# State-space block on one Trainium2 core: weighted sums in one phase a unit later, full-height small matmuls, and normalisation on ScalarE

## The chip, the cores and the metric

The kernel runs on one core of a Trainium2 chip. The core has five engines with a queue of instructions each, which it executes in order: TensorE (PE in the profile; PEld is its loading of stationary operands), VectorE (DVE), ScalarE (ACT), GpSimd (POOL) and SyncE (SP), which here issues the DMA transfers. Engines wait for each other by semaphores. SBUF is the working memory of 128 partitions; PSUM, in banks of 512 fp32 numbers per partition, takes the results of TensorE. The metric is the device time of one execution in microseconds.

## The reference

The input `x` is 4 x 4096 x 512 in fp32. A Mamba block with a residual is followed by a spectral layer with a residual:

```python
x = x + mamba(layernorm(x))        # D_INNER 1024, 16 states, conv of 4 taps, DT_RANK 32
x = x + ffn(layernorm(x))          # ifft(fft(x) @ w), real part, plus bias

# mamba, per time step:
u, z = split(x @ W_in.T);  u = silu(conv4(u) + conv_b)
dt_r, B, C = split(u @ W_x.T)      # 32, 16, 16
dt = softplus(dt_r @ W_dt.T + b_dt)
h  = exp(dt * A) * h + (dt * u) * B      # one state of 16 numbers for each of 1024 channels
y  = sum over the states of h * C
out = ((y + u * D) * silu(z)) @ W_out.T
```

The part that matters here is `h` (a recurrence along time for each channel and state) and `y`, the sum of `h` over the 16 states, weighted by `C`.

## The kernel before, in words

The 4 x 4096 rows are cut into 32 chunks of T = 512 time steps. In a chunk the 1024 channels are 8 blocks `d` of 128 partitions, and the 16 states are 4 groups `q` of four. One **unit** is one (chunk, d, q): there are 32 x 8 x 4 = 1,024 of them, and the main loop goes through them in order.

Four steps make a unit:

- `scans` (L451 on): POOL forms `bh` = du * B for 128 channels x 512 steps x 4 states (L455). For each of the four states ACT computes the decay `a` = exp(dt * A) into one of two PSUM tiles (L97, by way of L459), and DVE scans along time (L461). POOL then keeps the last column as `carry` (L464). Three `bh` buffers rotate (BH = 3).
- `contract` (L467 on), one unit behind the scans: the 512 steps are taken in four blocks `tt` of 128 steps. TensorE transposes four slices of 32 steps x 4 states into one of two PSUM tiles `tr` (L479); ACT copies them to SBUF as `hT` (L481); four matmuls with the mask of `C`, 32 columns wide each, sum over the states into `yT` (L483). These four stand at different columns of the array (`tile_position`). An fp32 matmul of this kind shows as two instructions in the trace, a transpose as one. A `yT` accumulates over the four `q` of a `d`; there is one PSUM buffer for it. The state tile `bh` comes free after its last transpose.
- `gate` (L499 on), after the fourth `q` of a block: ACT copies `yT` to `ys` (L505), TensorE transposes it back (L510), DVE adds `u * D` (L512), which releases the `ur` tile, and POOL multiplies by the gate `zr` (L519) that SP has loaded (L503).
- `prep` (L419 on), issued six units ahead: SP loads `ur` (L422); TensorE computes dt's input `v` from a full matmul (L426) and a correction with 32 rows (L427); ACT and POOL make softplus and `du` of it (L429 to L447).

`make_C` (L412 on) forms the masks of `C` for the next chunk with a 32-row matmul (L414) and a product on DVE (L416). `normalize` (L214 on) computes mean and variance on DVE, the inverse root on ACT and small DVE operations (L228 to L230), and applies them on POOL (L232). It serves the 128 input tiles (four at a time, in `load_norm`) and the 128 tiles of the second layernorm (one at a time, in `out_norm`).

All other work is "background": the input projection of the next chunk (`project`, matmuls at L332, weights by SP), output projection and spectral layer of the chunk before (L539, L573). In each unit `run_step` goes through four ticks. In each tick it takes one step of `contract` and one of `scans`, then steps of pending gates, then as much background work as two budgets allow (L686 to L722). A scheduler at build time then fixes the order on each engine from the dependencies and its own estimates; `add_manual_dep` adds an order between two instructions without a semaphore.

The loop calls the units like this:

```python
for i in range(NCH):
    for d in range(ND):
        for q in range(NQ):
            ...
            run_step((i, d, q), prev, share)
            prev = (i, d, q)
run_step(None, prev, (0.0, 0.0))
```

Of the kernel before, what the change touches and what calls it, by code (L numbers as in the profile page):

```python
# [8 lines left out]
F32 = mybir.dt.float32  # L9
F32R = mybir.dt.float32r  # L10
AF = mybir.ActivationFunctionType
ALU = mybir.AluOpType
# [4 lines left out]
P = 128  # L17
T = 512
M = 512
KM = M // P  # L20
DI = 1024
ND = DI // P
NS = 16
NQ = 4
# [7 lines left out]
XL = 2  # L32
AB = 2
PH = 2
HT = 4
BH = 3
CB = 4
TMP = 4
# [27 lines left out]
def tile_mamba_block(  # L66
# [108 lines left out]
    wx = cst.tile([P, ND, P], F32, name="wx")  # L175
    rc = cst.tile([P, 3], F32, name="rc")
    wv = cst.tile([P, DI], F32R, name="wv")
    wl = cst.tile([96, DI], F32R, name="wl")
    selt = wl[64:96, 0 : NQ * P].rearrange("s (q p) -> s q p", p=P)
    bias_bc = cst.tile([P, M], F32, name="bias_bc")  # L180
    dmask = cst.tile([P, 32], F32, name="dmask")
    carry = cst.tile([P, ND, NS], F32, name="carry")
# [11 lines left out]
    def consts2():  # L194
        nc.sync.dma_start(A, a_log)
        lut(A, A, AF.Exp)
        nc.vector.tensor_scalar(A, A, -1.0, None, ALU.mult)
        nc.sync.dma_start(dsk, d_skip)
        nc.sync.dma_start(dmask, diag)
        nc.sync.dma_start(bias_bc, bias.to_broadcast([P, M]))  # L200
        wvr = p_bh.tile([P, 2, DI], F32, name="wvr", tag="bh")
        nc.gpsimd.memset(wvr[:, 0, :], 0.0)
        nc.sync.dma_start(wvr[0:32, 0, :], w_dt_t)
        nc.sync.dma_start(wvr[32:64, 0, :], w_dt_t)
        nc.sync.dma_start(wvr[112:113, 0, :], b_dt)
        nc.sync.dma_start(wvr[113:114, 0, :], b_dt)
        nc.sync.dma_start(wvr[64:96, 1, 0 : NQ * P], sel.rearrange("s q p -> s (q p)"))
        nc.vector.tensor_copy(wl[64:96, 0 : NQ * P], wvr[64:96, 1, 0 : NQ * P])
        wvh = p_bh.tile([P, 2, DI], F32R, name="wvh", tag="bh")
        nc.scalar.activation(wvh[:, 0, :], wvr[:, 0, :], AF.Copy)  # L210
        nc.vector.scalar_tensor_tensor(wv, wvh[:, 0, :].bitcast(F32), rc[:, 2:3], wvr[:, 0, :], ALU.mult, ALU.add)
        nc.vector.tensor_tensor(wl[0:32, :], wvr[0:32, 0, :], wvh[0:32, 0, :].bitcast(F32), ALU.subtract)

    def normalize(srcs, dsts):  # L214
        n = len(srcs)
        st = p_sm.tile([P, n, 6], F32, name="st", tag=f"st{n}", bufs=SMB)
        mv = p_sm.tile([P, n, 2], F32, name="mv", tag=f"mv{n}", bufs=SMB)
        for k, src in enumerate(srcs):
            nc.vector.bn_stats(st[:, k, :], src)
            nc.vector.bn_aggr(mv[:, k, :], st[:, k, :])  # L220
        ve = p_sm.tile([P, n], F32, name="ve", tag=f"ve{n}", bufs=SMB)
        nc.vector.tensor_scalar(ve, mv[:, :, 1], EPS, None, ALU.add)
        rs = p_sm.tile([P, n], F32, name="rs", tag=f"rs{n}", bufs=SMB)
        lut(rs, ve, AF.Ln)
        lut(rs, rs, AF.Exp, scale=-0.5)
        for k in range(n):
            v, r = ve[:, k : k + 1], rs[:, k : k + 1]
            nc.vector.tensor_scalar(v, v, r, r, ALU.mult, ALU.mult)  # L228
            nc.vector.tensor_scalar(v, v, -0.5, 1.5, ALU.mult, ALU.add)
            nc.vector.tensor_scalar(r, r, v, None, ALU.mult)  # L230
        for k, (src, dst) in enumerate(zip(srcs, dsts)):
            nc.gpsimd.tensor_scalar(dst, src, mv[:, k, 0:1], rs[:, k : k + 1], ALU.subtract, ALU.mult)  # L232

    S = {i: {} for i in range(-1, NCH + 1)}

# [175 lines left out]

    def make_C(i, q):  # L412
        pc = ps_ph.tile([P, T // 32, 32], F32, name="pc", tag="ph")
        nc.tensor.matmul(pc, selt[:, q, :], S[i]["stk"][64:96, :], start=True, stop=True)  # L414
        cm = p_C.tile([P, T // 32, 32], F32, name="cm")
        nc.vector.tensor_tensor(cm, pc, dmask.unsqueeze(1).to_broadcast([P, T // 32, 32]), ALU.mult)  # L416
        S[i]["C", q] = cm

    def prep(i, d):  # L419
        st = S[i]  # L420
        u = p_ur.tile([P, T], F32, name="ur")
        nc.sync.dma_start(u, st["us"][d])  # L422
        st["u", d] = u
        v = ps_ph.tile([P, T], F32, name="v", tag="ph")
        ds = slice(d * P, (d + 1) * P)
        nc.tensor.matmul(v, wv[:, ds], st["stk"], start=True, stop=False)  # L426
        nc.tensor.matmul(v, wl[0:32, ds], st["stk"][0:32, :], start=False, stop=True)  # L427
        e = p_tmp.tile([P, T], F32, name="e", tag="tmp")
        nc.scalar.activation(e, v, AF.Abs)  # L429
        r = p_tmp.tile([P, T], F32, name="r", tag="tmp")  # L430
        nc.scalar.activation(r, v, AF.Relu)  # L431
        lut(e, e, AF.Exp, scale=-1.0)
        yield
        w = p_tmp.tile([P, T], F32, name="w1", tag="tmp")
        nc.gpsimd.tensor_scalar(w, e, 1.0, -1.0, ALU.add, ALU.add)  # L435
        l = p_tmp.tile([P, T], F32, name="l", tag="tmp")
        lut(l, e, AF.Ln, bias=1.0)
        yield
        nc.gpsimd.tensor_tensor(e, e, w, ALU.subtract)  # L439
        yield  # L440
        nc.gpsimd.tensor_tensor(l, l, e, ALU.add)
        yield
        dt = p_dt.tile([P, T], F32, name="dt")
        nc.gpsimd.tensor_tensor(dt, r, l, ALU.add)
        yield
        du = p_dt.tile([P, T], F32, name="du")
        nc.gpsimd.tensor_tensor(du, dt, u, ALU.mult)  # L447
        st["dt", d] = dt
        st["du", d] = du
# [14 lines left out]
            nc.gpsimd.tensor_copy(carry[:, d, 4 * q : 4 * q + 4], bh[:, T - 1, :])  # L464
        st["h", d, q] = bh

    def contract(i, d, q):  # L467
        st = S[i]
        bh = st.pop(("h", d, q))
        if q == 0:  # L470
            st["y", d] = ps_y.tile([P, T // P, P], F32, name="yT")
            st["first"] = {}
        yT = st["y", d]
        cm = st["C", q]
        for tt in range(T // P):
            tr = ps_tr.tile([P, 4, P], F32, name="tr")
            for j in range(4):
                t0 = (tt * 4 + j) * 32
                nc.tensor.transpose(tr[:, j, :], bh[:, t0 : t0 + 32, :].rearrange("p t s -> p (t s)"), ident)  # L479
            hT = p_hT.tile([P, 4, P], F32, name="hT")  # L480
            nc.scalar.activation(hT, tr, AF.Copy)  # L481
            for j in range(4):
                ins = nc.tensor.matmul(  # L483
                    yT[32 * j : 32 * j + 32, tt, :],
                    cm[:, tt * 4 + j, :],
                    hT[:, j, :],
                    start=(q == 0 and tt == 0),
                    stop=(q == NQ - 1),
                    skip_group_check=True,
                    tile_position=(0, 32 * j),  # L490
                )
                if q == 0:
                    if tt == 0:
                        st["first"][j] = ins.ins
                    else:
                        tc.add_manual_dep(ins.ins, st["first"][j].name, NOSYNC, reason="bank start first")
            yield

    def gate(i, d):  # L499
        st = S[i]  # L500
# [184 lines left out]

    def run_step(cur, prev, share):  # L686
        gens = []
        if prev is not None:
            gens.append(contract(*prev))
        if cur is not None:  # L690
            gens.append(scans(*cur))
        if SC1:
            gens.reverse()
        if prev is not None and prev[1] == ND - 1 and prev[0] + 1 < NCH:
            make_C(prev[0] + 1, prev[2])
        for _ in range(4):
            tick[0] += 1
            if PSTEP and tick[0] % PSTEP == 0:
                for g in list(soon):
                    if next(g, "end") == "end":  # L700
                        soon.remove(g)
            for what in SLOT:
                if what == "m":
                    for g in gens:
                        next(g, None)
                elif what == "g":
                    for g in list(late):
                        if next(g, "end") == "end":
                            late.remove(g)
                elif what == "a":  # L710
                    bga.advance(share[0] / 4)
                else:
                    bgb.advance(share[1] / 4)
        for g in gens:
            next(g, None)
        if cur is not None and cur[1] == ND - 1 and cur[0] + 1 < NCH:
            load_B(cur[0] + 1, cur[2])
        if prev is not None and prev[2] == NQ - 1:
            i, d = prev[0], prev[1]
            bgb.until(lambda: ("z", d) in S[i])  # L720
            bga.until(lambda: len(yz_free) >= 2)
            late.append(gate(i, d))  # L722
# [5 lines left out]
# [3 lines that stand above are left out]
# [13 lines left out]
                run_step((i, d, q), prev, share)  # L744
                prev = (i, d, q)
    run_step(None, prev, (0.0, 0.0))
    for g in late:
        run(g)
    for g in (bgb, bga):
# [66 lines left out]
```

## Time and profile before

| | us |
|---|---|
| median of 3 runs | 8955.14 (8951.78 to 8959.92) |
| the profiled execution, its own time | 8950.2 |
| its span, first to last instruction | 8948.4 |
| busy: PE / POOL / DVE / ACT | 7853.7 / 6985.1 / 6652.0 / 6460.5 |
| mean granted TensorE clock | 0.938 |
| DMA, mean over the span | 152 GB/s |

A row of the groups names the line, the engine, the operation, the tiles written and read, the shape and the number of instructions; then their busy time together and the mean duration of one in ns; then the idle time of the engine just before them, with what ended it. A row of the waits gives who waited for whom, the total, how often and the longest. A row of the timeline gives start and length of a stretch of equal instructions. Matmuls overlap each other in these rows, so costs are read from one start to the next rather than from the lengths.

### The profile page before, as it was taken

Reading aid. Unit: us, or ns where it says so; the run is one execution under the profiler, and the core shown is the slowest. Engines: PE = TensorE matmul, PEld = TensorE weight load, DVE = VectorE, ACT = ScalarE, POOL = GpSimd, SP = SyncE. Lnnn points to the kernel's source line nnn. Section 1 sums busy time; section 2 is a strip of 40 time slices with the busy share of each in tenths; the row PEclk is TensorE's granted clock in tenths of the full one; section 3 lists DMA queues with packets and bytes.
Section 4 is the critical chain, followed back from the end, with each engine's and each line's share of the span. In section 5 each row is a group of like instructions: output and inputs, shape, how many; then the busy total and the mean of one; then the engine's idle time right before and its main releaser. Section 6 shows DMA issues by size and latency. Waiting matters only on the chain. (4 is left out here: it accounts for less than half of the span.)

```text
span 8948.4 us, 163408 instructions
## 1 busy us (share of the span) xinstructions
PE 7853.7 (88%) x62400; PEld 4812.5 (54%) x62400; DVE 6652.0 (74%) x7776; ACT 6460.5 (72%) x11199; POOL 6985.1 (78%) x4484
## 2 busy tenths in 40 slices
PE   7998888888888888898888898888988888888888
PEld 4555555555555555555555555555555555555554
DVE  5677777777777777777777777777777777777776
ACT  5777777777777777777677776777767777777775
POOL 5777778777778787887777887788778788778786
PEclk9999999999999999999999999999999999999999
DMA  7544444444444444444444444444444344444444
GB/s 236 161 161 155 154 139 144 150 156 154 143 145 154 151 160 144 144 147 159 155 150 142 143 152 154 158 143 149 148 151 161 132 151 147 162 155 152 142 148 145
DMA packets 615138, 1363.45 MB, mean 152 GB/s; under 512 B 126066, under 2 KB 138482, under 8 KB 597972
## 3 DMA queue, kind: packets, MB, share of 16 engines
q1 hardware_dynamic: 614356, 1353.00, 46.0%
q8 instruction: 494, 8.09, 0.4%
q14 instruction: 288, 2.36, 0.1%
HBM read 1171.38 MB, written 181.40 MB: 151 GB/s over the span
## 5 line engine op out<-in xcount | busy, mean ns | idle before, releaser
L461 DVE TENSOR_TENSOR_SCAN bh<-a,carry,bh 128x512 f32<-128x512 f32 x3584 | 4397.1, 1270 | 918.2 <-POOL bh L455 556.0
L455 POOL TENSOR_TENSOR bh<-du,bq 128x2048 f32<-128x2048 f32 x1024 | 3970.1, 3879 | 710.3 <-PE tr L479 675.8
L97 ACT ACTIVATE a<-dt,A 128x512 f32<-128x512 f32 x4096 | 2822.9, 694 | 1056.2 <-DVE bh L461 1038.0
L481 ACT ACTIVATE hT<-tr 128x512 f32<-128x512 f32 x4096 | 2388.0, 594 | 862.7 <-PE tr L479 847.4
L479 PE MATMUL tr<-ident,bh 128*128 128x128 f32 x16384 | 2813.4, 299 | 220.9 <-ACT hT L481 110.5
L479 PEld LDWEIGHTS tr<-ident,bh 128*128 128x128 f32 x16384 | 1844.7, 148 | 1067.5 <-issue 906.9
L483 PE MATMUL yT<-hT,cm 128*32 128x128 f32 x32768 | 1804.4, 295 | 565.3 <-ACT hT L481 507.7
L483 PEld LDWEIGHTS yT<-hT,cm 128*32 128x32 f32 x32768 | 662.1, 110 | 1732.1 <-ACT hT L481 948.5
L332 PE MATMUL pp<-xh,w 128*128 128x512 f32 x4096 | 1467.7, 421 | 17.1 <-ACT r L431 6.6
L539 PE MATMUL po<-wo,yz 128*128 128x512 f32 x2048 | 957.3, 597 | 22.0 <-DVE xr L576 9.1
L332 PEld LDWEIGHTS pp<-xh,w 128*128 128x128 f32 x4096 | 812.2, 199 | 220.0 <-issue 14.0
L332 PE MATMUL pp<-xl,w 128*128 128x512 f32 x2048 | 836.6, 409 | 7.2 <-DVE xl L296 7.1
L461 DVE TENSOR_TENSOR_SCAN bh<-a,bh 128x512 f32<-128x512 f32 x512 | 594.9, 1209 | 167.0 <-POOL bh L455 91.3
L464 POOL COPY carry<-bh 128x4 f32<-128x4 f32 x896 | 182.0, 203 | 532.0 <-DVE bh L461 506.5
L435 POOL TENSOR_SCALAR w<-e 128x512 f32<-128x512 f32 x256 | 495.1, 1934 | 116.1 <-ACT e L97 116.0
L343 DVE SCALAR_TENSOR_TENSOR u<-pp,cw,u 128x509 f32<-128x509 f32 (+2 forms) x768 | 565.7, 737 | 11.6
L519 POOL TENSOR_TENSOR yz<-g,zr 128x256 f32<-128x256 f32 x512 | 368.8, 741 | 250.8 <-DVE g L512 193.1
L539 PEld LDWEIGHTS po<-wo,yz 128*128 128x128 f32 x2048 | 359.2, 191 | 332.2 <-issue 291.9
L332 PEld LDWEIGHTS pp<-xl,w 128*128 128x128 f32 x2048 | 408.1, 199 | 91.7 <-DVE xl L296 11.1
L573 PE MATMUL pf<-g,x1t 128*128 128x512 f32 x1024 | 370.9, 443 | 85.6 <-DMA g<-g_split 51.9
L512 DVE SCALAR_TENSOR_TENSOR g<-ur,dsk,yt 128x512 f32<-128x512 f32 x256 | 188.2, 735 | 249.9 <-ACT hT L481 106.6
L439 POOL TENSOR_TENSOR e<-e,w 128x512 f32<-128x512 f32 x256 | 330.1, 1289 | 40.3 <-ACT l L97 38.5
(86 smaller groups left out, 6814.3 us busy)
## 6 DMA issues: line engine op xcount, KB each, us to landing
wo<-w_out_t SPq DMA_DIRECT2D x516, 512.0 KB, 4.9
g<-g_split SPq DMA_DIRECT2D x512, 512.0 KB, 4.0
w<-w_split SPq DMA_DIRECT2D x496, 512.0 KB, 3.4
bq<-bsc SPq DMA_DIRECT2D x128, 1024.0 KB, 4.9
xr<-x SPq DMA_DIRECT2D x256, 256.0 KB, 3.2
usc<-u SPq DMA_DIRECT2D x256, 256.0 KB, 2.9
ur<-usc SPq DMA_DIRECT2D x256, 256.0 KB, 2.7
zsc<-u SPq DMA_DIRECT2D x256, 256.0 KB, 2.5
```

The costliest lines, as they stand in the source:

```text
L97: ins = nc.scalar.activation(out_, in_, func, **kw)
L332: nc.tensor.matmul(ps, w[:, wsel, k, :], xt[:, k, :], start=(n == 0), stop=(n == 3 * KM - 1))
L343: nc.vector.scalar_tensor_tensor(u[:, j:], ps[:, : T - j], cw[:, d, 3 - j : 4 - j], u[:, j:], ALU.mult, ALU.add)
L435: nc.gpsimd.tensor_scalar(w, e, 1.0, -1.0, ALU.add, ALU.add)
L455: nc.gpsimd.tensor_tensor(bh, st["du", d].unsqueeze(2).to_broadcast([P, T, 4]), st["B", q], ALU.mult)
L461: nc.vector.tensor_tensor_scan(bh[:, :, j], a, bh[:, :, j], init, ALU.mult, ALU.add)
L479: nc.tensor.transpose(tr[:, j, :], bh[:, t0 : t0 + 32, :].rearrange("p t s -> p (t s)"), ident)
L481: nc.scalar.activation(hT, tr, AF.Copy)
L483: ins = nc.tensor.matmul(yT[32 * j : 32 * j + 32, tt, :], cm[:, tt * 4 + j, :], hT[:, j, :], start=(q == 0 and tt == 0), stop=(q == NQ - 1 ...
L519: nc.gpsimd.tensor_tensor(yz, g[:, hs], zr[:, hs], ALU.mult)
L539: nc.tensor.matmul(po, yz_of(i, d, tt), wo[:, d % 2, :], start=(d == d0), stop=(d == d1 - 1))
L573: nc.tensor.matmul(pf, a[:, k, :], g[:, b, :], start=(k == 0 and m == 0), stop=(k == KM - 1 and m == 2))
```

## The change

Three things change. (1) `contract` is split. It still transposes and copies a unit's four blocks, but keeps the four `hT` tiles in `held`; a new function `weigh` does the sixteen weighted sums of the unit before, all in a row, after the first block's transposes. Manual dependencies place them after that block and ahead of the second block's transposes. `hT` has five buffers in place of four. `gate` and `make_C` follow the unit that was weighed, so they move a unit later, and one more step stands at the end. (2) The constants `selt` and `wl` are filled with zeros to 128 rows, and the matmuls at L414 and L427 take all 128 rows of `stk`. (3) `normalize` applies mean and inverse root with an Identity activation on ACT, scale `r` and bias `-m * r`; the bias is one more small DVE operation for each tile.

```diff
-HT = 4
+HT = 5
@@
-    wl = cst.tile([96, DI], F32R, name="wl")
-    selt = wl[64:96, 0 : NQ * P].rearrange("s (q p) -> s q p", p=P)
+    wl = cst.tile([P, DI], F32R, name="wl")
+    selt = cst.tile([P, NQ, P], F32R, name="selt")
@@ consts2
+        nc.gpsimd.memset(wvr[:, 1, 0 : NQ * P], 0.0)
         nc.sync.dma_start(wvr[64:96, 1, 0 : NQ * P], sel.rearrange("s q p -> s (q p)"))
-        nc.vector.tensor_copy(wl[64:96, 0 : NQ * P], wvr[64:96, 1, 0 : NQ * P])
+        nc.vector.tensor_copy(selt.rearrange("s q p -> s (q p)"), wvr[:, 1, 0 : NQ * P])
...
-        nc.vector.tensor_tensor(wl[0:32, :], wvr[0:32, 0, :], wvh[0:32, 0, :].bitcast(F32), ALU.subtract)
+        nc.gpsimd.memset(wvr[:, 1, :], 0.0)
+        nc.vector.tensor_tensor(wvr[0:32, 1, :], wvr[0:32, 0, :], wvh[0:32, 0, :].bitcast(F32), ALU.subtract)
+        nc.vector.tensor_copy(wl, wvr[:, 1, :])
@@ normalize
-            nc.gpsimd.tensor_scalar(dst, src, mv[:, k, 0:1], rs[:, k : k + 1], ALU.subtract, ALU.mult)
+            m, r = mv[:, k, 0:1], rs[:, k : k + 1]
+            nc.vector.tensor_scalar(m, m, r, -1.0, ALU.mult, ALU.mult)
+            nc.scalar.activation(dst, src, AF.Identity, scale=r, bias=m)
@@ make_C, prep
-        nc.tensor.matmul(pc, selt[:, q, :], S[i]["stk"][64:96, :], start=True, stop=True)
+        nc.tensor.matmul(pc, selt[:, q, :], S[i]["stk"], start=True, stop=True)
...
-        nc.tensor.matmul(v, wl[0:32, ds], st["stk"][0:32, :], start=False, stop=True)
+        nc.tensor.matmul(v, wl[:, ds], st["stk"], start=False, stop=True)
@@ contract
+    held = []
+
+    def weigh(after):
+        i, d, q, blocks = held.pop()
+        st = S[i]
+        if q == 0:
+            st["y", d] = ps_y.tile([P, T // P, P], F32, name="yT")
+        yT = st["y", d]
+        cm = st["C", q]
+        prev = after
+        for tt, hT in enumerate(blocks):
+            for j in range(4):
+                ins = nc.tensor.matmul(
+                    yT[32 * j : 32 * j + 32, tt, :],
...
+                ).ins
+                if prev is not None:
+                    tc.add_manual_dep(ins, prev.name, NOSYNC, reason="one phase")
+                prev = ins
+        return prev, (i, d, q)
+
+    def contract(i, d, q, done):
+        st = S[i]
+        bh = st.pop(("h", d, q))
+        blocks = []
+        after = None
+        for tt in range(T // P):
+            tr = ps_tr.tile([P, 4, P], F32, name="tr")
+            for j in range(4):
+                t0 = (tt * 4 + j) * 32
+                ins = nc.tensor.transpose(tr[:, j, :], bh[:, t0 : t0 + 32, :].rearrange("p t s -> p (t s)"), ident).ins
+                if after is not None:
+                    tc.add_manual_dep(ins, after.name, NOSYNC, reason="one phase")
+                    after = None
+            hT = p_hT.tile([P, 4, P], F32, name="hT")
+            nc.scalar.activation(hT, tr, AF.Copy)
+            blocks.append(hT)
+            if tt == 0 and held:
+                after, unit = weigh(ins)
+                done.append(unit)
             yield
+        held.append((i, d, q, blocks))
@@ run_step
-        if prev is not None and prev[1] == ND - 1 and prev[0] + 1 < NCH:
-            make_C(prev[0] + 1, prev[2])
+        if prev is None and held:
+            done.append(weigh(None)[1])
...
-        if prev is not None and prev[2] == NQ - 1:
-            i, d = prev[0], prev[1]
+        for i, d, q in done:
+            if d == ND - 1 and i + 1 < NCH:
+                make_C(i + 1, q)
+            if q < NQ - 1:
+                continue
             bgb.until(lambda: ("z", d) in S[i])
             bga.until(lambda: len(yz_free) >= 2)
             late.append(gate(i, d))
@@
     run_step(None, prev, (0.0, 0.0))
+    run_step(None, None, (0.0, 0.0))
```

More of the change, by code (lines that the diff above doesn't have):

```diff
@@ L465, in scans @@
         st["h", d, q] = bh
-    def contract(i, d, q):
+    held = []
+    def weigh(after):
+        i, d, q, blocks = held.pop()
         st = S[i]
-        bh = st.pop(("h", d, q))
         if q == 0:
             st["y", d] = ps_y.tile([P, T // P, P], F32, name="yT")
-            st["first"] = {}
         yT = st["y", d]
         cm = st["C", q]
[L475 to L481, printed above, removed]
+        prev = after
+        for tt, hT in enumerate(blocks):
             for j in range(4):
@@ L490, in contract @@
                     tile_position=(0, 32 * j),
[L491 to L496, printed above, removed]
+                ).ins
[22 more added lines that the diff above has]
+                done.append(unit)
             yield
+        held.append((i, d, q, blocks))
     def gate(i, d):
@@ L687, in run_step @@
         gens = []
+        done = []
         if prev is not None:
-            gens.append(contract(*prev))
+            gens.append(contract(*prev, done))
         if cur is not None:
```

## The prediction

> **What bounds the kernel now.** I read the page's busy shares first, then the waits of TensorE, then the timeline of TensorE in steady state, then the groups of the lines that the diff touches.
>
> ```profile
> PE 7853.7 (88%) x62400; PEld 4812.5 (54%) x62400; DVE 6652.0 (74%) x7776; ACT 6460.5 (72%) x11199; POOL 6985.1 (78%) x4484
> ```
>
> No engine is full, but TensorE is nearest to it: 7854 of 8948 us, alike in all slices. There are 1,024 units (32 chunks x 8 channel blocks x 4 state groups), so a unit takes 8948.4 / 1024 = 8.74 us, and of that TensorE is busy 7.67, POOL 6.82, DVE 6.50 and ACT 6.31.
>
> What TensorE waits for, longest first (total us, times, longest):
>
> ```profile
> PE yT L483 <- ACT hT L481: 507.7, 452, 5.6
> PE tr L479 <- ACT hT L481: 110.5, 85, 5.6
> PE tr L479 <- DVE bh L461: 106.7, 88, 6.6
> PE pf L573 <- DMA g<-g_split: 51.9, 55, 4.2
> PE yT L483 <- ACT ys L505: 38.5, 72, 1.1
> ```
>
> Of 8948 - 7854 = 1095 us idle, 508 are the weighted sums waiting for the copy of the block just transposed. DVE's scans hold TensorE up for only 107. In the other direction POOL's product waits 676 us for TensorE to release a state tile (idle of L455 below). So the ring POOL - DVE - TensorE - POOL is held mainly at TensorE.
>
> How TensorE spends its time around the change (start us, duration):
>
> ```profile
> 4011.38 0.43 PE L483 MATMUL yT<-hT,cm 128*32 128x128 f32 x8
> 4011.74 0.66 PE L479 MATMUL tr<-ident,bh 128*128 128x128 f32 x4
> 4012.32 0.42 PE L483 MATMUL yT<-hT,cm 128*32 128x128 f32 x8
> 4012.68 1.11 PE L479 MATMUL tr<-ident,bh 128*128 128x128 f32 x8
> 4013.73 0.42 PE L483 MATMUL yT<-hT,cm 128*32 128x128 f32 x8
> ...
> 4014.49 0.47 PE L426 MATMUL v<-stk,wv 128*128 128x512 f32 x1
> 4014.90 0.49 PE L427 MATMUL v<-stk,wl 32*128 32x512 f32 x1
> 4015.32 0.43 PE L483 MATMUL yT<-hT,cm 128*32 128x128 f32 x8
> ...
> 4019.01 0.39 PE L332 MATMUL pp<-xl,w 128*128 128x512 f32 x1
> 4019.24 0.39 PE L332 MATMUL pp<-xh,w 128*128 128x512 f32 x1
> 4019.56 0.42 PE L483 MATMUL yT<-hT,cm 128*32 128x128 f32 x8
> ```
> ```profile
> 214.44 0.64 PE L483 MATMUL yT<-hT,cm 128*32 128x128 f32 x16
> 215.01 0.77 PE L479 MATMUL tr<-ident,bh 128*128 128x128 f32 x5
> ```
>
> Read the starts. Eight yT instructions and the step out take 4011.74 - 4011.38 = 0.36; sixteen take 215.01 - 214.44 = 0.57. So eight more cost 0.21, and 0.36 - 0.21 = **0.15 us is paid for leaving** the 32-column form. Four transposes and the step into yT take 0.58, eight take 4013.73 - 4012.68 = 1.05: four more cost 0.47 (0.44 at the 0.11 us of a long run), so **0.11 to 0.14 is paid for entering**. One phase of weighted sums thus costs 0.26 to 0.29 us beside its work. I take 0.28.
>
> The groups that the diff touches (busy, mean ns | idle before):
>
> ```profile
> L455 POOL TENSOR_TENSOR bh<-du,bq 128x2048 f32<-128x2048 f32 x1024 | 3970.1, 3879 | 710.3 <-PE tr L479 675.8 <-issue 15.5 <-ACT u L114 5.4
> L97 ACT ACTIVATE a<-dt,A 128x512 f32<-128x512 f32 x4096 | 2822.9, 694 | 1056.2 <-DVE bh L461 1038.0 <-DVE ve L229 2.3 <-DVE ve L222 1.0
> L481 ACT ACTIVATE hT<-tr 128x512 f32<-128x512 f32 x4096 | 2388.0, 594 | 862.7 <-PE tr L479 847.4 <-ACT hT L481 0.6
> L232 POOL TENSOR_SCALAR xr<-xr,mv,rs 128x512 f32<-128x512 f32 x128 | 266.4, 2093 | 28.3 <-DVE rs L230 15.3 <-ACT a L97 11.4 <-ACT hT L481 1.6
> L427 PE MATMUL v<-stk,wl 32*128 32x512 f32 x256 | 129.8, 507 | 0.0
> L426 PE MATMUL v<-stk,wv 128*128 128x512 f32 x256 | 126.8, 495 | 16.0 <-DVE stk L394 12.4 <-DVE g L512 2.6 <-ACT r L431 0.3
> ```
>
> **The change part by part.** The sum goes against the profiled execution: 8950.2 us, span 8948.4 and 1.8 around it. The median of the runs shown, 8955.14, is 4.9 (0.05%) above it. Two results less than 0.2% apart can't be told from no change.
>
> *Phases.* All 16,384 transposes and 16,384 weighted sums stay; only their order changes. In the instruction order of the built programs the weighted sums stand in 3,999 unbroken runs before (nearly all of four matmuls, which the trace shows as eight instructions) and in 1,412 after (672 of sixteen, most others split into twelve and four). So 2,587 phases go: x 0.28 us = 724 us at full clock. The mean granted clock of the run was 0.938 (view of cores), so these steps lasted somewhat longer: / 0.938 = 772. By the bounds 0.26 and 0.29: 715 to 800. **-770.**
>
> *Padding to 128 rows.* The 32-row matmul takes as long as the 128-row one (507 against 495 ns mean). But the pair L426, L427 takes 4015.32 - 4014.49 = 0.83 us, where two full matmuls of this kind and the step into yT would take 2 x 0.23 + 0.09 = 0.55 (the projection's matmuls at L332 start 0.23 apart, 4019.01 to 4019.24, and yT starts 0.32 after the last, so 0.09 is the step in). That is 0.28 for each of 256, 72 us; L414's 128 I price alike, 36 us. Bounds: 0 (the step only moves elsewhere) to 0.37 each (no yT behind), 142. With the clock, **-110.** The Trainium skill (TensorEngine Tiling (Array Packing), Performance Considerations) speaks against this: a contraction of 32 rows should be packed four to the array for up to 4x, so padding would give up as much as three quarters of 384 x 0.23 = 66 us, and the forecast would be 8,226 in place of 8,050. But packing needs other 32-row matmuls beside it, and the timeline shows each of these alone between full ones.
>
> *The wait for hT.* A unit later, the weighted sums find their blocks copied: up to 508 + 38 us of waits go. What is late next: a transpose writes one of two PSUM tiles, so the third and fourth of a unit, and the first of the next, wait for copies two groups back. In the new order about 2,900 transpose groups wait on ACT, against some 220 before, while yT groups that do fall from 4,096 to 1,031. Two groups of lead in place of one halves the need, I estimate, rather than ends it. Bounds: -546 and +250 (half of the 508 added instead). I take the middle of the half removed: **-250.**
>
> *DVE next.* With TensorE about 0.9 us a unit shorter, DVE (6652 us) and ACT stand closer to the bound, and TensorE will more often wait for a scan. Before that cost 107. Bounds: 0 to 700 (DVE's own idle behind POOL and ACT, 647 and 427, two thirds of which stay). I take **+250**, nearer to the row.
>
> *Normalising on ScalarE.* POOL loses 256 x 2.09 = 533 us. ACT gains 256 passes of 128x512 with two per-partition operands: nearest rows 594 (none) and 694 (one), so about 0.79 each, 203 us (bounds 0.59, and 0.89 with three such steps: 152 and 228). DVE gains 256 one-column operations like L228 to L230 (144 to 263 ns), 37 to 67 us. ACT now waits where POOL waited for DVE (53 + 15 us), and exps and copies queue behind it. Against that POOL's product, for which DVE waits 647, no longer queues behind up to four 2.1 us passes. Neither engine is the bound, so **0**, with -150 to +150.
>
> *Moved a unit later.* Gate: its copy ys, four yt transposes, L512, two POOL products and SP's zr load all go past one unit's work. The ur tile is released by L512, so SP's ur load, which stands in order with the weight loads, comes 8 us later; du needs it only when a dt tile comes free, and that wait was 0.2 us. Cover: the dt wait. If it went, du and the next product would slip by up to 8 us per block. make_C keeps its lead of four units. At the end one more phase, at the start two memsets of 1 us and a longer constant chain: +3 together, with no DMA added.
>
> Sum: -770 - 110 - 250 + 250 + 0 + 3 = -877 on the span. 8948.4 - 877 + 1.8 = 8073; since the waits removed also shorten POOL's 676 us stall and the cold stretches behind stalls, I round down to **8,050**, 7.86 us a unit. TensorE would be busy about 6,970 us, 87%.
>
> **The rivals.**
> 1. *Another ring takes over.* ACT's exps wait 1038 us for scans and its copies stand behind them; DVE needs 6,710 us. For: all four engines would lie at 80% or more. Against: their idle is largely spent on TensorE (847 and 676 us). If half of the 877 is given back: 8,510; 8,400 to 8,930.
> 2. *Slower: transposes stall on ACT.* If a copy queued behind an exp that waits for its scan holds the two PSUM tiles, TensorE stops with all its background matmuls behind. The wait for hT went by 4,096 groups at 508 / 4096 = 0.12 us each. The matmul savings of 880 plus the 508 removed are used up when 2,900 transpose groups wait 0.48 us each; at 0.7 us the time is 8950 - 1388 + 2030 = 9,590. For: a copy is 0.59 us, and a transpose group 0.44, so two adjacent groups don't cover one. Against: the built order puts other matmuls, or the phase of 1 us, between most pairs.
> 3. *The drains don't go.* The phases may only move the cost: 12 of 16 sums run, then 4 wait. Then only waits change: 8,700 to 8,950, about no change.
>
> **How the numbers follow.** Forecast case (7,650 to 8,400): 0.68. Rival 1: 0.15. Rival 3: 0.05, with 0.02 of it within 0.2% of 8955. Rival 2: 0.12 (8,970 to 9,600). Faster 0.68 + 0.15 + 0.03 = 0.86, same 0.02, slower 0.12. Low end: the larger bounds of phases, hT wait and normalising with DVE's +250 give -800 - 140 - 546 - 100 + 250 = -1336, 7,614; I take 7,640. High end: rival 1 to its middle, 8,600; above it lie rival 2, rival 3 and a third of rival 1, some 0.2. The likeliest case alone: 7,700 to 8,400.
>
> **What would show it.** Right: unbroken rows of 32 yT instructions, 1.0 to 1.1 us long; L483's idle behind hT below 150 us; TensorE's busy time near 6,970; POOL without the normalising rows and its wait for tr well under 676; ACT at about 6,660. Wrong: tr waiting for hT over 600 us (rival 2); scans waiting for exps over 700 (rival 1); sixteen-row phases as long as four phases of four (rival 3). The forecast fails most easily in the +250 given to DVE, which no row of before fixes.

## The result

The changed kernel takes 9033.17 us (median; 9022.6 to 9042.35) against 8957.53 before: ratio 1.0084, 95% interval 1.0066 to 1.0101. It is **slower by 0.8%**, where 10% faster was forecast. The profiled execution took 9022.6 with a span of 9020.5.

The first line of the page of the changed kernel, busy time of each engine and its share of the span:

```profile
PE 7221.9 (80%) x62400; PEld 5114.6 (57%) x62400; DVE 6690.3 (74%) x8033; ACT 6616.6 (73%) x11455; POOL 6458.1 (72%) x4230
```

TensorE lost 632 us of busy time and POOL 527, ACT gained 156, and yet the span grew by 72. So TensorE, POOL and DVE are idle longer than before; ACT alone is idle 84 us less. TensorE's idle time went from 1095 to 9020.5 - 7221.9 = 1799 us. The waits of TensorE in the changed kernel (total us, times, longest):

```profile
PE tr L507 <- ACT hT L512: 470.0, 538, 5.7
PE yT L484 <- ACT ys L526: 464.0, 75, 10.9
PE pt L583 <- ACT x1n L237: 191.5, 55, 9.3
PE yT L484 <- ACT hT L512: 151.1, 137, 3.6
PE tr L507 <- DVE bh L466: 62.8, 52, 3.8
```

Two things stand out. The wait for `hT` has changed its place, from the sums (508) to the transposes (470), and is hardly smaller: 618 us before, 621 now. And the wait of the sums for `ys`, 38 us before, is now 464, in pieces of up to 10.9 us. Of its 75 pieces, 32 are longer than 8 us, one in each chunk, and these make 347 us of it. I had written that this wait goes.

One such piece in the timeline of TensorE of the changed kernel (start, length, idle before):

```profile
4014.16 1.08 PE L484 MATMUL yT<-hT,cm 128*32 128x128 f32 x32
4015.17 0.66 PE L507 MATMUL tr<-ident,bh 128*128 128x128 f32 x4
...
4020.44 0.63 PE L507 MATMUL tr<-ident,bh 128*128 128x128 f32 x4 [0.96 <-ACT hT L512]
4031.97 1.94 PE L484 MATMUL yT<-hT,cm 128*32 128x128 f32 x32 [10.90 <-ACT ys L526]
4033.84 1.97 PE L507 MATMUL tr<-ident,bh 128*128 128x128 f32 x8
```

The phase itself does what was worked out: 32 instructions and the step out take 4015.17 - 4014.16 = 1.01 us, where four phases of eight took 4 x 0.36 = 1.44. At 4015.17 the block's `yT` is finished. TensorE reaches the next block's first sums at about 4021 and finds the only `yT` buffer still not copied out; it stands until 4031.97. What ACT and POOL did meanwhile, in the same kernel:

```profile
4013.42 0.59 ACT L434 ACTIVATE e<-v 128x512 f32<-128x512 f32 x1
4013.90 0.60 ACT L436 ACTIVATE r<-v 128x512 f32<-128x512 f32 x1
...
4017.07 0.66 ACT L97 ACTIVATE l<-e 128x512 f32<-128x512 f32 x1
...
4025.82 1.28 ACT L114 ACT_TABLE_LOAD   x1
4027.12 2.19 ACT L114 ACTIVATE u<-u 128x512 f32<-128x512 f32 x4
4029.32 1.28 ACT L104 ACT_TABLE_LOAD   x1
...
4031.34 0.58 ACT L526 ACTIVATE ys<-yT 128x512 f32<-128x512 f32 x1
```
```profile
4018.10 1.92 POOL L440 TENSOR_SCALAR w<-e 128x512 f32<-128x512 f32 x1
...
4023.95 1.28 POOL L444 TENSOR_TENSOR e<-e,w 128x512 f32<-128x512 f32 x1
```

`e`, `r`, `l` and `w` are prep's four tiles, and the pool `tmp`, from which `ys` takes its tile too, has four buffers. The first to come free is `w`, when L444 ends at 4025.2. By then ACT's next work is the silu burst, four silu passes in a row between two loads of ACT's function tables (4025.82 to 4030.6), and the copy comes at 4031.34, 16 us after its sums were done. ACT is not idle before it: at run time the copy doesn't wait for a buffer, it stands in ACT's queue behind other work, in the order that the scheduler fixed at build time. Over the whole run 52 of the 256 copies start more than 8 us after their sums (at most 16.5); in the kernel before none does. In the kernel before, the gate was a unit earlier and wrote `ys` and `g` before prep took its tiles. That gives the first theory to test: **the change moves the gate behind prep in the rotation of a buffer pool.**

### The profile page after: what moved, and what is told of

The parts are those of the page before. It is cut to its first block, busy times and chain, and to the rows that moved or that the text cites. A ratio compares the mean times of both kernels' runs of the same rounds, so it can differ in the third digit from the quotient of the medians.

```text
span 9020.5 us, 163087 instructions
## 1 busy us (share of the span) xinstructions
PE 7221.9 (80%) x62400; PEld 5114.6 (57%) x62400; DVE 6690.3 (74%) x8033; ACT 6616.6 (73%) x11455; POOL 6458.1 (72%) x4230
## 4 chain that ended last, share of the span: by engine, by line
DVE 29%; PE 23%; ACT 19%; POOL 16%; issue 8%; DMA 5%; SPq 0%; POOLq 0%; ACTq 0%; DVEq 0%
DVE bh L466 22%; POOL bh L460 12%; PE tr L507 6%; ACT a L97 5%; PE pp L337 5%; ACT hT L512 5%; PE yT L484 4%; PE po L560 3%; ACT u L114 2%; DVE u L348 2%; PE pf L594 2%; ACT L114 2%; ACT L104 2%; DMA g<-g_split 1%; DMA xr<-x 1%
## 5 line engine op out<-in xcount | busy, mean ns | idle before, releaser
L507 PE MATMUL tr<-ident,bh 128*128 128x128 f32 x16384 | 2522.0, 292 | 611.6 <-ACT hT L512 470.0
L512 ACT ACTIVATE hT<-tr 128x512 f32<-128x512 f32 x4096 | 2321.4, 594 | 601.9 <-PE tr L507 586.5
L507 PEld LDWEIGHTS tr<-ident,bh 128*128 128x128 f32 x16384 | 1941.8, 148 | 1300.5 <-ACT hT L512 543.9
L484 PE MATMUL yT<-hT,cm 128*32 128x128 f32 x32768 | 1329.5, 295 | 616.1 <-ACT ys L526 464.0
L484 PEld LDWEIGHTS yT<-hT,cm 128*32 128x32 f32 x32768 | 878.3, 116 | 1050.8 <-ACT ys L526 487.4
L560 PE MATMUL po<-wo,yz 128*128 128x512 f32 x2048 | 1017.5, 620 | 51.7 <-DVE xr L597 30.2
L337 PEld LDWEIGHTS pp<-xh,w 128*128 128x128 f32 x4096 | 784.6, 193 | 267.0 <-issue 39.4
L449 POOL TENSOR_TENSOR dt<-r,l 128x512 f32<-128x512 f32 x256 | 330.4, 1291 | 510.3 <-ACT a L97 340.6
L348 DVE SCALAR_TENSOR_TENSOR u<-pp,cw,u 128x511 f32<-128x511 f32 (+2 forms) x768 | 564.5, 738 | 13.0
L452 POOL TENSOR_TENSOR du<-dt,ur 128x512 f32<-128x512 f32 x256 | 329.6, 1288 | 81.0 <-DMA ur<-usc 77.8
```

The source lines that it names most:

```text
L337: nc.tensor.matmul(ps, w[:, wsel, k, :], xt[:, k, :], start=(n == 0), stop=(n == 3 * KM - 1))
L348: nc.vector.scalar_tensor_tensor(u[:, j:], ps[:, : T - j], cw[:, d, 3 - j : 4 - j], u[:, j:], ALU.mult, ALU.add)
L484: ins = nc.tensor.matmul(yT[32 * j : 32 * j + 32, tt, :], cm[:, tt * 4 + j, :], hT[:, j, :], start=(q == 0 and tt == 0), stop=(q == NQ - 1 ...
L507: ins = nc.tensor.transpose(tr[:, j, :], bh[:, t0 : t0 + 32, :].rearrange("p t s -> p (t s)"), ident).ins
L560: nc.tensor.matmul(po, yz_of(i, d, tt), wo[:, d % 2, :], start=(d == d0), stop=(d == d1 - 1))
```

## The experiments

Each was run beside the kernel before, whose medians lay between 8,957 and 8,965. Ratios are to it, with 95% intervals.

| run | what it is | us | ratio |
|---|---|---|---|
| changed | | 9033 | 1.0084 (1.0066 to 1.0101) |
| e1 | changed, ys copied early | 8634 | 0.9630 (0.9613 to 0.9646) |
| e2 | changed, normalising on POOL | 9162 | 1.0223 (1.0207 to 1.0238) |
| e3 | phases alone | 9193 | 1.0257 (1.0241 to 1.0272) |
| e4 | padding alone | 8921 | 0.9953 (0.9938 to 0.9968) |
| e5 | changed, tile of ys early, copy late | 9027 | 1.0077 (1.0060 to 1.0095) |
| e6 | changed, five tmp buffers, no padding | 8721 | 0.9738 (0.9718 to 0.9759) |
| e7 | e1, normalising on POOL | 8878 | 0.9902 (0.9886 to 0.9919) |
| e8 | phases alone, ys copied early | 8891 | 0.9920 (0.9905 to 0.9935) |
| e9 | normalising on ACT alone | 8855 | 0.9880 (0.9866 to 0.9895) |
| e10 | padding and normalising on ACT | 8839 | 0.9864 (0.9849 to 0.9879) |
| e11 | before, 470 us of TensorE's work left out | 8835 | 0.9856 (0.9839 to 0.9872) |
| e12 | e1, the same left out | 8486 | 0.9470 (0.9456 to 0.9484) |
| e13 | changed, prep a unit later | 8430 | 0.9409 (0.9395 to 0.9423) |
| e14 | e1, 377 us of DVE's work left out | 8563 | 0.9558 (0.9542 to 0.9574) |
| e15 | before, prep a unit later | 9052 | 1.0103 (1.0088 to 1.0118) |
| e16 | e1 and e13 together | 8427 | 0.9405 (0.9389 to 0.9421) |

### The copy early, and the parts

e1 writes the copy behind the weighing instead of in the gate:

```diff
                 after, unit = weigh(ins)
                 done.append(unit)
+                copy_out(*unit)      # if q == NQ - 1: ys = p_tmp.tile(...); activation(ys, yT, AF.Copy)
@@ gate
-        ys = p_tmp.tile([P, T // P, P], F32, name="ys", tag="tmp")
-        nc.scalar.activation(ys, yT, AF.Copy)
+        ys = st.pop(("ys", d))
```

> The changed kernel, with the copy of yT to ys (ACT) written right behind the weighing of a block's last unit, so that it takes its tile of the four-buffer pool tmp before the next prep's four tiles do, as it did in the kernel before. Theory (rotation): in the changed kernel the copy takes its tile behind prep's, so it is held until POOL releases one and then stands behind ACT's silu burst; the single yT buffer makes TensorE stand 464 us behind it. Then TensorE's wait for ys falls from 464 to under 100 us and the time from 9033 to 8,550 to 8,750. Rival A (order on ACT): the copy is held by the exps and the burst wherever it is written; the wait stays over 250 us and the time over 8,930. Rival B (TensorE no longer the bound): the wait goes, but the time stays over 8,900 because the waits move to DVE and ACT.

Measured 8634, which is 399 us below the changed kernel and inside the theory's range. The waits of TensorE in e1:

```profile
PE tr L513 <- ACT hT L518: 288.3, 408, 5.7
PE tr L513 <- DVE bh L466: 197.0, 97, 3.9
PE tr L513 <- issue: 95.8, 80, 4.1
PE yT L484 <- ACT hT L518: 83.1, 97, 3.7
```

The sums no longer appear behind `ys`, and no copy starts more than 5.4 us after its sums. Rivals A and B fall.

e2 puts L232 back in place of the three lines of `normalize`; e3 also takes back the padding; e4 is the kernel before with the padding lines of the diff.

> The changed kernel with normalisation put back on POOL. Theory: normalising on ACT costs TensorE 192 us behind the normalised tile in the second layernorm and delays exps and copies, so without it the time falls by 50 to 200, to 8,830 to 8,980; POOL's busy time rises by about 530 to 6,990. Rival (POOL's relief is what holds the changed kernel up to the level of the kernel before): the time rises by 50 or more, above 9,080. Both may be hidden behind the stall on ys: then within 30 us of 9033.

> The kernel before with the weighing a unit later in one phase alone (five hT buffers, no padding, normalisation on POOL). Theory (rotation): the stall on ys is there in full, 350 to 550 us; TensorE's busy time falls by 500 to 700 from 7854; the time lies between 8,900 and 9,100. Rival: the stall comes with the normalisation on ACT, whose passes lengthen ACT's queue; then the wait for ys is under 150 us here and the time 8,450 to 8,700.

> The kernel before with the padding of the small matmuls to 128 rows alone. Prediction's term: 110 us off TensorE's busy time and as much off the time, 8,840 to 8,880. Rival: padding moves nothing that lies on the path, or the scheduler's new order costs as much: the time within 0.3% of before, 8,930 to 8,985.

e2 went against the theory and as its rival had it: normalising on ACT is worth 9162 - 9033 = **129 us**, although TensorE waits 191 us for `x1n` because of it. e3 shows the stall without the other two parts: 9193, above the range given, with TensorE's busy time only 438 us lower (7853.7 to 7415.9), where 500 to 700 were expected. This is its wait of TensorE:

```profile
PE yT L479 <- ACT ys L521: 604.1, 116, 10.9
```

So the phases as they stand cost 9193 - 8965 = 228 us and bring the stall (its rival, that the stall comes with normalising on ACT, falls). e4 saved 44 us of time for 92 of TensorE's busy time (7853.7 to 7761.9); the prediction's term had 80 to 120 of time, and the rival no more than 30, so it lies between the two. On top of other parts the padding is worth less: 31 us (e3 to e2), 16 (e9 to e10) and 13 (e8 to e7).

### Rotation of the pool, or order of writing?

e1 moves both the tile and the instruction. Four runs separate them:

```diff
 # e5: the tile is taken in copy_out, the copy stays in gate
 # e6: TMP = 4 -> 5 (the padding is taken back to make room in SBUF)
 # e13, e15: PL = 6 -> 5, in the changed kernel and in the kernel before: prep is written a unit later
 # e16: e1 with PL = 5
```

> The changed kernel, with the tile of ys taken early (behind the weighing, ahead of the next prep's four tiles of the pool tmp) but its copy written where the changed kernel has it, in the gate. Theory (rotation of tmp): holding the place in the rotation is enough; TensorE's wait for ys stays under 120 us and the time is 8,600 to 8,720, as with the early copy (8,634). Rival (order of writing): the scheduler lets ACT do first what is written first, so the copy again stands behind the exps and the silu burst; the wait is 300 us or more and the time over 8,900.

> The changed kernel with five tiles in the pool tmp in place of four, and, to make room for it in SBUF, without the padding to 128 rows (which was worth 31 and 44 us where it was alone). The copy is written late, as in the changed kernel. Theory (rotation): a fifth tile lets the copy go while prep holds four, so the wait for ys falls below 150 us and the time to 8,630 to 8,760. Rival (order of writing): the wait for ys stays over 300 us and the time over 8,950.

> The changed kernel with PL = 5 in place of 6: the preparation of a block is written one unit later, so the gate's ys and g again come ahead of prep's four tiles in the pool tmp. The copy stays written where the changed kernel has it, behind the same exps and the same silu burst. Theory (rotation of tmp, places taken in the order of the first writes): TensorE's wait for ys falls from 464 to under 150 us, the time to 8,600 to 8,780, unless the later preparation makes scans wait. Rival (order of writing on ACT): the wait stays over 300 us, the time over 8,900.

> The kernel before with PL = 5: control for the run above (8,430). Theory (rotation): in the kernel before ys and g already come ahead of prep with PL = 6, so moving prep a unit later mends nothing and shortens its lead: 8,900 to 9,100. Rival: the later preparation is better in itself, whatever the gate does: below 8,800, and most of the 600 us between 9,033 and 8,430 are not the rotation's.

> The changed kernel with both: the copy of yT written early and PL = 5. Theory (rotation): with prep a unit later ys and g both come ahead of its tiles, so writing the copy early adds nothing, 8,400 to 8,470. Rival (two separate gains, the order of writing and the lead of prep): they add up, below 8,300.

e5 changed nothing: 9027, with 463.6 us of waiting in 74 pieces against 464.0 in 75. Taken alone it speaks for the order of writing. e6 speaks against that: with a fifth buffer and the copy written as late as ever, TensorE's wait for `ys` falls to 16 us and the time to 8721, inside the theory's range, though the padding is missing. It does not bring every copy forward: 23 of the 256 still start more than 8 us after their sums (at most 10.4). The longest waits of TensorE in e6 are for `hT` and scans:

```profile
PE tr L504 <- ACT hT L509: 491.7, 430, 7.2
PE tr L504 <- DVE bh L463: 118.1, 75, 3.9
PE yT L481 <- ACT hT L509: 111.0, 73, 3.9
```

e13 points the same way. With prep one unit later, `ys` and `g` are again written before prep's four tiles, while the copy stays written where the changed kernel has it. (Prep's own four ACT passes, some 2.5 us together, come behind the copy too, so it is e6 that separates the buffers from the order of writing.) The time is **8430, 603 us below the changed kernel** and below its range of 8,600 to 8,780. Its waits of TensorE hold no `yT` behind `ys` at all:

```profile
PE tr L507 <- ACT hT L512: 440.9, 509, 5.1
PE yT L484 <- ACT hT L512: 241.6, 149, 6.3
PE tr L507 <- issue: 148.2, 97, 8.0
PE tr L507 <- DVE bh L466: 106.0, 99, 3.0
PE yt L531 <- ACT ys L526: 65.5, 73, 5.9
```

The control e15 shows that it isn't the later preparation in itself: in the kernel before, where the gate already came ahead, the same constant costs 1.0%. And e16 shows that e1 and e13 mend the same thing, since together they give 8427. So what holds the copy is the gate's place behind prep, and the number of buffers in the pool decides how much that costs. That a place is taken with the first write and not where the tile is asked for is my reading of e5; it wasn't looked at directly. e13 gains 204 us more than e1. In e1 only `ys` is ahead of prep's tiles and `g` still behind them, which is a possible reason; no run isolates it.

### What TensorE's work is worth

The forecast counted a microsecond of TensorE's work as a microsecond of time. e7 to e12 and e14 test that.

> The early copy (8,634) with normalisation back on POOL. With the stall in place normalising on ACT was worth 129 us. Theory: it is worth as much without it, since POOL stands nearer to the bound: 8,710 to 8,800. Rival: with the copies of yT on time ACT is the dearer place, and the time falls below 8,620.

> The weighing in one phase a unit later with the early copy, without padding and with normalisation on POOL. This is the prediction's first and third term without the stall. Theory: the phases alone save 120 to 250 of before's 8,960, 8,710 to 8,840, with TensorE's busy time at about 7,400. Rival (forecast's size right, the other parts cost time): below 8,500.

> The kernel before with normalisation on ACT alone. Theory (uneven stages): once a chunk five normalising passes and two others stand together on POOL for 11.5 us ahead of the next state tile, and that unit lasts 23.4 us from first scan to first scan where DVE's scans need 5. Off POOL, that unit falls to 9 to 13 us, and 32 chunks give 300 to 450 us: 8,510 to 8,660. Rival (busy shares): neither POOL at 78% nor ACT at 72% is the bound, so nothing: 8,900 to 9,010. A third reading, that ACT's passes hold up exps and copies, ends above 9,010.

> Padding and normalisation on ACT without the phases. Theory (uneven stages): 40 below the run with normalisation alone, 8,470 to 8,620, at or below the 8,634 of the whole change with the early copy: then the phases themselves, a unit late, are worth nothing or cost time. Rival (phases carry the gain): 8,750 or more, the phases being worth over 100.

> The kernel before without the product of W_in's upper half with x's lower half (xl) in the projection: 2,048 of TensorE's matmuls of 0.23 us are left out, 470 us of its work, and nothing else. This tests the assumption under the forecast, that time follows TensorE's work. Forecast's assumption: 380 to 480 us off, 8,480 to 8,580. Theory (uneven stages: many units are as short as DVE's scans allow, others stand behind POOL or ACT): less than half of it, 50 to 230 us off, 8,730 to 8,910.

> The changed kernel with the early copy (8,634), without the same 2,048 matmuls of the projection (470 us of TensorE's work left out). Theory: with the phases TensorE is still further from the bound, so less comes off than from the kernel before, 0 to 150 us: 8,480 to 8,640. Rival: TensorE is the bound again once the POOL stretch is gone, 300 us or more: below 8,330.

> The changed kernel with the early copy (8,634), without two of the three shifted taps of the convolution: 512 of DVE's operations of 0.74 us are left out, 377 us of its work. Reading 1 (the prediction's rival 1: another ring, through DVE's scans, now sets the time): most of it comes off, 250 to 380 us, 8,250 to 8,390. Reading 2 (no single engine is the bound, stages of a chunk have different ones): about as small a share as for TensorE's work, 40 to 160 us, 8,470 to 8,600.

```diff
 # e11, e12 (project)
-            for wsel, xt in ((0, xh), (0, xl), (1, xh)):
+            for wsel, xt in ((0, xh), (1, xh)):
 # e14 (project)
-            for j in (1, 2, 3):
+            for j in (1,):
```

With 470 us of TensorE's work left out, the kernel before gets faster by 8960.3 - 8834.7 = 126 us (**27%**), and e1 by 8634.4 - 8485.7 = 149 (**32%**); both lie in the ranges of their theories. TensorE's busy time fell by less than 470: by 359 (7853.7 to 7494.4) and 394 (7249.7 to 6856.2), while the mean granted clock went from 0.938 to 0.920 and 0.927, so by busy time the shares are 35 and 38%. DVE's work is worth less still: 71 of 377 us (19%), as reading 2 had it. So neither TensorE nor DVE alone sets the time of e1. ACT's work was not tested in this way, and POOL's only by moving the normalisation.

One stretch that another engine holds can be seen in the trace of before. Two windows, each with its length, then the busy time of PE, PEld, DVE, ACT and POOL, then clock and DMA:

```profile
4008.00:4013.00 5.00, 4.51 (x59) 2.78 (x60) 0.20 (x1) 3.74 (x8) 5.00 (x3) 1.00 0.00 0
4013.00:4021.74 8.74, 8.05 (x70) 5.36 (x67) 0.78 (x2) 3.42 (x8) 8.74 (x5) 1.00 0.23 67
```

In these 13.7 us POOL is full and DVE does next to nothing. TensorE is 91% busy as well, but it isn't what makes the unit long: in e11, without 470 us of its work, this unit, the fifth of its chunk, still has a median of 23.8 us over the chunks. The timelines of POOL and DVE say why:

```profile
4003.19 8.26 POOL L232 TENSOR_SCALAR xr<-xr,mv,rs 128x512 f32<-128x512 f32 x4 [0.78 <-ACT a L97]
4011.43 2.08 POOL L232 TENSOR_SCALAR x1n<-xr,mv,rs 128x512 f32<-128x512 f32 x1
4013.47 1.27 POOL L441 TENSOR_TENSOR l<-l,e 128x512 f32<-128x512 f32 x1
4014.70 3.87 POOL L455 TENSOR_TENSOR bh<-du,bq 128x2048 f32<-128x2048 f32 x1
```
```profile
4003.41 4.80 DVE L461 TENSOR_TENSOR_SCAN bh<-a,carry,bh 128x512 f32<-128x512 f32 x4
...
4021.70 0.69 DVE L296 TENSOR_TENSOR xl<-pt,xh 128x512 fp32r<-128x512 f32 x1 [6.12 <-ACT xh L295]
...
4026.76 2.43 DVE L461 TENSOR_TENSOR_SCAN bh<-a,carry,bh 128x512 f32<-128x512 f32 x2
```

Five normalising passes keep POOL from the next product until 4014.7, and this unit lasts 4026.76 - 4003.41 = 23.4 us from scan to scan. POOL explains it only up to 4018.6, when the product is done. For the other 8.2 us the scan stands in DVE's queue behind work on the tiles just normalised (L296, which waited 6.12 us for ACT's `xh`, and what follows it). A unit whose four scans follow each other takes about 5. The mean of 8.74 on which the forecast rests describes neither. Such a unit comes once a chunk, nearly always as the fifth, whose median is 23.2 us in the kernel before.

Normalising on ACT removes that stretch: in e9 the fifth unit has a median of 7.1 us. It saved 105 us alone (e9), 82 on top of the padding (e4 to e10), 129 in the changed kernel (e2), and 8878 - 8634 = **244 with the early copy** (e7; its theory had 80 to 170). It is the largest gain of the change, where the forecast had 0. e9 came short of the 300 to 450 that its theory took from the 23.4 us unit. Two waits of DVE, in before and then in e9:

```profile
DVE bh L461 <- POOL bh L455: 647.2, 276, 11.9
DVE xl L296 <- ACT xh L295: 204.2, 67, 6.3
```
```profile
DVE bh L463 <- POOL bh L457: 837.2, 339, 5.8
DVE xl L298 <- ACT xh L297: 25.6, 19, 3.7
```

The long pieces are gone, but the scans wait for POOL's product more often and 190 us longer in all. The time came back in the units behind: the median of the fifth fell by 16 us, those of the sixth to eighth rose from 6.2, 7.8 and 8.3 to 10.4, 11.9 and 13.2.

The phases with the early copy are worth 8839 - 8634 = 205 us (e10 to e1) with normalising on ACT, and with it on POOL 72 without the padding (e8) and 43 with it (e4 to e7). So the theory of e10, that they are worth nothing, fell too, and e8 saved less than the 120 to 250 that its theory had. TensorE's busy time fell by 478, 455 and 495 us in these three pairs, so a microsecond of it was worth 0.43, 0.16 and 0.09 us: there is no one price for it. The phases and normalising on ACT are worth more together than apart.

## Why the prediction was wrong, step by step

- **Moved a unit later.** This step failed, and it turned the gain into a loss. I followed the gate past one unit's work, SP's load and the dt tiles, and named `ys` as a wait that goes. I didn't ask what the gate passes in the pools it takes tiles from. `ys` and `g` come from the same four buffers as prep's tiles, and a unit later the gate stands behind prep. TensorE's sums then waited 464 us for `ys` in place of 38, and putting the gate ahead again gained 399 (e1, `ys` alone) to 603 us (e13).
- **What bounds the kernel.** "The ring is held mainly at TensorE" failed, and with it the size of every TensorE term. 88% busy was an average over stretches with different bounds; a microsecond less of TensorE's busy time was worth 0.09 to 0.48 us in the pairs above, not 1. Even without the stall the whole change reached 8634 or 8430, not 8,050. The evidence lay in the trace of before, in the windows above, which I had read for TensorE alone.
- **Phases.** The work was right: the traces show 3,999 and 1,412 unbroken rows of sums, and the tr and yT groups fell from 2813.4 + 1804.4 to 2522.0 + 1329.5 us, by 766 (forecast 770). The time was 205, 72 or 43. TensorE as a whole lost only 632 of the 880 us forecast, as rows of other matmuls grew (po from 957 to 1017 us) and the clock fell to 0.917.
- **Padding.** 92 us of busy time against 110, and 13 to 44 of time. (36 + 72 us over the clock of 0.938 would have been 115.) The matmul at L432 now takes 410 ns where L427 took 507. The Trainium skill (TensorEngine Tiling (Array Packing), Performance Considerations) recommends 4x row tiling for a contraction of 32 rows, and the prediction estimated from it that padding would lose 66 us. For 32-row matmuls that stand alone this case shows a gain instead; packed ones were not tried.
- **The wait for hT.** The 250 us did not come: 618 us before, 621 after. In e1, free of the stall, it is 371, and in e13, also free of it and faster, 682.
- **DVE next.** I had reserved 250 us. In e1 TensorE waits 197 us for scans, 90 more than before. That was an extra term in a sum whose base was wrong.
- **Normalising.** The forecast had 0 with bounds of 150 either way; the runs show gains of 82 to 244 us. The hint lay in the 647 us that DVE waits for POOL, quoted in that very step: not the total, which rose in e9, but its longest piece of 11.9 us, which fell to 5.8.
- **Rivals.** Rival 2 named the right kind of ending (TensorE standing behind a copy on ACT with all else behind it), at 0.12, but with the wrong buffer: the transposes behind `hT` rather than the sums behind `ys`. Rival 1's range holds e1, e8 and e13, but no single ring was found to have taken over (e14). Rival 3 is out: sixteen sums take 1.01 us, not 1.44. The low end of the range was added up with 100 for normalising although its bound was 150; with that it would have been 7,564 and not 7,614.
- **The signs.** Those named for being right mostly came: rows of 32, the sums' wait for `hT` at 151 us (150 was the limit), ACT at 6617, POOL's wait for `tr` at 417 in place of 676. Only TensorE's busy time missed, 7222 for 6,970. None of the three signs of being wrong did. No sign watched the wait for `ys`, so the list would have passed a kernel that is slower.

Left open: what holds e13 at 8430. No single wait in its profile accounts for it; the order within the chunk would have to be taken apart stretch by stretch.

## What to carry to other kernels

When a step is moved later, list every pool from which it takes a tile and see which other users of that pool it now comes behind, not only whose data it needs; here a copy whose data were ready came 16 us late. Before a busy share is turned into time, look at single units: here they lasted between 5 and 23 us, and the largest gain came from taking away the 23. And where a change that should help is level or slower, its parts are worth running apart: here one constant (PL = 5) made 1.0084 into 0.9409.

## What the runs showed of the hardware

A stall of TensorE cost more than its length. The 32 sums after the 10.9 us wait took 1.94 us against 1.08 in the phase before it. The granted clock, as a share of full speed, was 1.00 from 4015 to 4021, 0.50 from 4032 to 4034, when these sums ran, and 1.00 again from 4036 on. Over whole runs, taking away the wait for `ys` raised the mean clock each time: 0.917 to 0.938 (e1) and 0.952 (e13), 0.909 to 0.918 (e3 to e8) and 0.909 to 0.924 (e2 to e7). That wait isn't all that lowers it, as e11, with 34 us of it, had 0.920.

Each per-partition operand of an ACT pass over 128x512 took some 0.09 us more. With the source in PSUM, passes took 594 ns with no such operand (`hT`) and 685 with one (`xd`); with source and result in SBUF, 618 to 636 with none (silu, exp, log) and 804 to 811 with two (normalising).
